# Row numbers in registers: SyncE fetches one tile in every fifth group row by row, in a graph layer's edge sums

## The chip, the cores and the metric

The kernel runs on one core of a Trainium2 chip. The metric is the device time in microseconds of one execution; it is given as the median of three. The five engines of the core are called by the profile's names: PE (matmuls; PEld are its weight loads), DVE, ACT, POOL (GpSimd) and SP (SyncE, which only issues DMAs and waits). A "q" behind an engine's name means its sequencer.

## The reference

One graph layer with 12500 nodes, 256 features and 200000 edges, sorted by destination:

```
h   = relu(layernorm(x))
agg = segment_sum(h[src], dst, 12500)
z   = (1 + eps) * h + agg
t   = relu(batchnorm(z @ W1 + b1))            # 256 -> 512
y   = relu(batchnorm(t @ W2 + b2 + h))        # 512 -> 256
out = x + y
```

The costly part ahead of the two products is `h[src]` with its sum: 200000 rows of 256 features, fetched by number.

## The kernel before, in words

**Tiles and groups.** 128 edges are a tile (1563 of them), and ten tiles a group (`GT`, 157 groups). For most groups POOL fetches the rows of `h` with one indirect DMA for each tile (`gather`, L653, issue at L665). DVE makes for each group a one-hot of destinations (`edges`, L716), and PE multiplies one-hot by rows, ten matmuls into one sum of 128 places (`sums`, L733, matmul at L748). `hold`, `spots`, `put` (L834) and `add` (L851) bring that sum to the right columns of `zc`, where z is built in chunks of 512 nodes. When a chunk is whole, `slice_of` (L861) multiplies it by W1 in four slices, and `take` (L872, L878) stores each slice to `t_tab` from SP (L879), out of one of two places called `ts`.

**Lead-in and table.** In the first 34 steps (`LEAD`) the gathered rows are rows of x, normalised on the core. Beside that the table `h_tab` is written: 2 KB a row, h in a rounded part and the rest. From step 34 on groups gather from `h_tab` into one of three places (`RING`), four steps ahead of their sums (`AHEAD`).

**Counted groups.** Two sets of 12 groups (`SETS`, `JOINT`) are not gathered at all. All of `h_tab` is read in order, in 98 blocks of 128 rows, into a ring of ten places (`h_loads`, the stream loads of SP at L963). A *unit* is one of these groups against eight blocks: DVE makes a one-hot of the high part of the source numbers (`marks`, `mk`, L991), PE multiplies it with a one-hot of the low part (`fill`, L1008), ACT copies the counts (L1012), PE weighs the blocks with them (`weigh`, L1024), and DVE adds the product up (`collect`, L1041). There are 312 units, 13 rounds for each set. The block at which a unit begins moves on by eight in twelve units.

**Homes.** The low one-hots (fp8, ten tiles of 128, 1280 bytes a partition) are made by `low_digits` (L973), one for each group of a set. Their *homes* lie in three places: `away` (three, `AWAY`), `w2s` (three; W2 is loaded later) and `spread` (twelve). The first homes of `spread` also hold the rows of one lead-in group until its sums. The second set takes over homes of the first; `again` and `early_digits` tell at which unit each is made anew. The first set's twelve are made in the last four lead-in steps, three in each.

**Order.** The order on each engine is written out by hand. Steps run through the gathered groups (`line`; the loop of L1175 has steps 34 to 127). `plan` spreads the units over the steps, with budgets for PE and DVE; `early_digits` is one of its costs. A step is a list `works`: units by turns with the group's sums, the placing of earlier sums, and slices. Each engine, SP too, works through its own instructions in the order of the program. SP has, in a step: loads of zc, then, in the places where units and slices stand, stream loads and stores to `t_tab`. A stream load waits until PE has weighed the block that had its place.

Of the kernel before, what the change touches and what calls it, by code (L numbers as in the profile page):

```python
# [9 lines left out]
F32 = mybir.dt.float32  # L10
F32R = mybir.dt.float32r
F8 = mybir.dt.float8e4
I32 = mybir.dt.int32
# [5 lines left out]
P = 128  # L19
# [5 lines left out]
LEAD = 34  # L25
# [7 lines left out]
JOINT = 12  # L33
# [2 lines left out]
PACE = 2  # L36
RINGS = 10
BUSY = 12500
AWAY = 3
EASE = 3  # L40


# [7 lines left out]
def kernel(  # L50
# [16 lines left out]
    nc = tc.nc  # L67
# [311 lines left out]
    def fast():  # L379
# [24 lines left out]
        with ExitStack() as fs:  # L404
# [14 lines left out]
            with ExitStack() as es:  # L419
# [222 lines left out]
                    nc.sync.dma_start(h_cols[g, :, :, :n], hc[:, :, :n])  # L642

                groups = [(t0, min(GT, NTILE - t0)) for t0 in range(0, NTILE, GT)]
                gathered = {i: early[i] for i in range(EARLY)}
                landing = [tc.alloc_semaphore(f"whole{k}") for k in range(AHEAD + 1 + RING)]
                inside = tc.alloc_semaphore("inside")
# [2 lines left out]
                def place_of(i):  # L650
                    return i % (AHEAD + 1) if i < LEAD else AHEAD + 1 + pos[i] % RING

                def gather(i):  # L653
                    t0, n = groups[i]
                    k = i % (AHEAD + 1)
                    if i >= LEAD:
                        pair = rows_pool.tile([P, 2 * GT, D], F32, name="gt")
                        ga = ((0, GT, pair.rearrange("p (t k) d -> p t (k d)", k=2)),)
                    elif k < EARLY:
                        ga = early[k]  # L660
                    else:
                        ga = ((0, GT, singles[k - EARLY]),)
                    for t in reversed(range(t0, t0 + n)):
                        rows = left if t == full_tiles else P
                        fetch = nc.gpsimd.indirect_dma_start(  # L665
                            out=slot(ga, t - t0)[:rows], out_offset=None, in_=x if i < LEAD else h_tab,
                            in_offset=bass.IndirectOffsetOnAxis(ap=srcT[:rows, t : t + 1], axis=0),
                        )
                        if i < NG - 2:
                            tc.no_tile_sem_insts.add(fetch.ins.name)  # L670
                            tc.add_to_no_dep_group(f"rows{i}", fetch.ins)
                            fetch.then_inc(inside if t > t0 else landing[place_of(i)], 16)
                    if i < NG - 2:
                        uses[place_of(i)] += 1
                        arrival[i] = landing[place_of(i)], 16 * uses[place_of(i)]
                    gathered[i] = ga
# [56 lines left out]
                def sums(i, among=()):  # L733

                    t0, n = groups[i]
                    ga, oh = gathered.pop(i), ohs.pop(i)
                    waited = wait_for(i, nc.tensor)
                    ps = sum_place(i)
                    order = list(reversed(range(n)))
                    at = {(k + 1) * n // (len(among) + 1): work for k, work in enumerate(among)}  # L740
                    for k, j in enumerate(order):
                        if k in at:
                            at[k]()
                        rows = left if t0 + j == full_tiles else P
                        lhsT, rhs, to = oh[:rows, j, :], slot(ga, j)[:rows], ps
                        if i >= LEAD:
                            lhsT, rhs, to = lhsT.bitcast(F32R), rhs.bitcast(F32R), ps.rearrange("p k d -> p (k d)")
                        reader = nc.tensor.matmul(to, lhsT=lhsT, rhs=rhs, start=(j == order[0]), stop=(j == order[-1]))  # L748
                        if waited:
                            behind(i, reader)  # L750
                            waited = False
                    summed[i] = ps
# [340 lines left out]
                for i in range(LEAD):  # L1093
                    before = added
                    c_now, c_last, c_next = (chunk_at.get(i + k) for k in (0, -1, 1))
                    gather(line[i + AHEAD])
                    if c_last is not None:
                        turn(c_last)
                    if i + 1 < LEAD:
                        scale("g", i + 1)  # L1100
                    if c_now is not None:
                        scale("c", c_now)
                    edges(line[i + FRONT])
                    if i >= 2:
                        spots(i - 2)
                        hold(i - 2)
                    if i + 1 < LEAD:
                        relus(gathered[i + 1], GT, gathered[i + 1], "g", i + 1)
                    if c_now is not None:
                        h_chunk(c_now)  # L1110
                    if i + 2 < LEAD:
                        look(gathered[i + 2], GT // 2, "g", i + 2)
                        root("g", i + 2)
                    if c_next is not None:
                        look_chunk(c_next)
                        root("c", c_next)
                    for c, f in taken:
                        take(c, f)
                    while added <= i - 4:
                        add(added)  # L1120
                        added += 1
                    if c_last is not None:
                        turn_out(c_last)
                    if c_now is not None:
                        h_halves(c_now)
                    for c in scales.get(i, ()):
                        z_scale(c)

                    def puts():
                        if i >= 3:  # L1130
                            put(i - 3)

                    while touching[whole][-1] < before:
                        queue += [(whole, f) for f in range(HC)]
                        whole += 1
                    taken = queue[:1]
                    queue = queue[1:]

                    def slice_ups():
                        for c, f in taken:  # L1140
                            slice_of(c, f)

                    for n in range(max(JOINT * (i - LEAD + 4) // 4, 0), JOINT * (i - LEAD + 5) // 4):
                        low_digits(n)
                    sums(i, (puts, slice_ups))
                    for c in loads.get(i, ()):
                        z_load(c)
# [27 lines left out]
                for s in range(LEAD, LAST):  # L1175
# [45 lines left out]
                    works = counting[:1] + others[:2]  # L1221
                    for k in range(1, max(len(counting), len(others) - 1)):
                        works += counting[k : k + 1] + others[k + 1 : k + 2]
                    for work in works:
                        work()
                    while whole < NCH and all(k in done for k in touching[whole]):
                        queue += [(whole, f) for f in range(HC)]
                        whole += 1
# [605 lines left out]
```

## Time and profile before

| | |
|---|---|
| median of three runs | 2436.89 us (2431.2, 2436.89, 2457.89) |
| the profiled execution | 2432.64 us, its span 2430.7 us |
| granted TensorE clock, mean | 0.879 |
| HBM read, written | 434.64 MB, 76.80 MB |
| q0, indirect DMAs of POOL: packets, MB, share of 16 engines | 94928, 302.21, 42.5% |
| gathers from h_tab (L665) | 983, 946 ns each |
| matmuls of the gathered sums (L748) | 970, 10 a group |
| units' weighing (L1024) | 2352 matmuls, 445 ns each |

All times are those of one profiled execution. A group row gives a source line, an engine, an operation with out<-in, a count, then busy time, the mean of one, and the engine's idle time just before them with what ended it ("<-issue": nothing that the profile shows). A row by source line gives minimum, median and maximum in ns and the first and last start. A row of the timeline gives start, length, engine, line and operation, and in brackets the idle time before. A row of waits on SP names SP's line, who ended the wait, the total, the number of waits and the longest.

### The profile page before, as it was taken

The page shows a single profiled execution, that of the slowest core. Times are in us where ns is not written, and L with a number is a line of the kernel's source. Part 1 is how long each engine was busy: PE and PEld are TensorE (multiplying, and loading weights), DVE is VectorE, ACT ScalarE, POOL GpSimd, SP SyncE. Part 2 cuts the span into 40 slices and gives each one's busy share as a digit, 9 for nine tenths or more (in the row PEclk, how much of TensorE's full clock was granted, in tenths as well). Part 3 has the DMA queues.
Part 4 walks back from the last instruction along what each step waited for, and adds up shares of the span by engine and source line. Part 5 has one row for each costly group of instructions (what it writes and reads, how often), then busy time and mean ns, then how long its engine had stood idle before and what let it go on. Part 6 is the DMA issues. An engine that isn't in the chain of part 4 may idle for free. (4 is left out here: it accounts for less than half of the span.)

```text
span 2430.7 us, 25628 instructions
## 1 busy us (share of the span) xinstructions
PE 1808.9 (74%) x8988; PEld 1277.0 (53%) x8988; DVE 1445.2 (59%) x2244; ACT 826.6 (34%) x1608; POOL 1332.5 (55%) x1372
## 2 busy tenths in 40 slices
PE   1566666637787788888786788788787877658997
PEld 1444444525565566556554556566565655425445
DVE  4565666636466565565556655555555655544897
ACT  1675656613322222222221222222222222112555
POOL 7666666653565555556545565555555545442550
PEclk9876887868998999899987899999898988689999
DMA  5667677656676766666666676676776756466888
GB/s 165 206 221 237 205 244 222 196 154 198 209 217 201 209 197 209 195 213 203 214 179 190 202 239 205 194 213 201 215 212 198 220 180 219 126 172 218 307 306 335
DMA packets 195410, 513.28 MB, mean 211 GB/s; under 512 B 30358, under 2 KB 45626, under 8 KB 195272
## 3 DMA queue, kind: packets, MB, share of 16 engines
q0 software_dynamic: 94928, 302.21, 42.5%
q1 hardware_dynamic: 98960, 208.29, 25.1%
q8 instruction: 73, 1.20, 0.2%
q10 hardware_dynamic: 1384, 1.06, 0.2%
q14 instruction: 65, 0.53, 0.1%
HBM read 434.64 MB, written 76.80 MB: 210 GB/s over the span
## 5 line engine op out<-in xcount | busy, mean ns | idle before, releaser
L665 POOL DMA_INDIRECT gt<-h_tab,srcT x983 | 930.2, 946 | 786.2 <-PE ps L748 453.4
L1024 PE MATMUL pz<-stream,counts 128*120 128x512 f32 (+1 forms) x2352 | 702.3, 445 | 26.5 <-issue 14.2
L1012 ACT CAST counts<-pm 128x480 fp32r<-128x480 f32 (+1 forms) x600 | 308.2, 556 | 843.9 <-PE pm L1008 387.0
L1024 PEld LDWEIGHTS pz<-stream,counts 128*120 128x120 f32 (+1 forms) x2352 | 453.7, 204 | 136.1 <-issue 17.3
L991 DVE SCALAR_TENSOR_TENSOR mk<-col,dstT 128x960 fp8e4<-128x960 f32 (+5 forms) x328 | 340.8, 1043 | 0.0
L1041 DVE TENSOR_TENSOR gta<-pz,gta 120x512 f32<-120x512 f32 x192 | 132.3, 689 | 325.4 <-PE pz L1024 198.2
L716 DVE TENSOR_TENSOR oh<-col,dstT 128x1280 fp32r<-128x1280 f32 (+1 forms) x131 | 194.2, 1483 | 150.3 <-remote 87.0
L748 PE MATMUL ps<-gt,oh 128*128 128x512 f32 x970 | 259.7, 417 | 0.0
L861 PE MATMUL ph<-zc,w1s 128*128 128x512 f32 (+1 forms) x392 | 207.0, 657 | 49.7 <-issue 19.1
L748 PEld LDWEIGHTS ps<-gt,oh 128*128 128x128 f32 x970 | 199.8, 207 | 49.5 <-issue 1.0
L1008 PE MATMUL pm<-mk,spread 128*128 128x96 fp8e4 (+1 forms) x1560 | 100.9, 210 | 115.8 <-issue 49.8
L1008 PEld LDWEIGHTS <-spread 128*128 128x128 fp8e4 x1560 | 79.8, 101 | 170.4 <-issue 109.9
L878 ACT COPY ts<-ph 128x512 f32<-128x512 f32 x96 | 56.0, 584 | 331.5 <-issue 176.4
L1041 DVE TENSOR_TENSOR gtb<-pz,gtb 120x512 f32<-120x512 f32 x96 | 66.1, 689 | 152.5 <-PE pz L1024 94.5
L665 POOL DMA_INDIRECT stream<-in_x_dram,srcT x130 | 124.3, 956 | 57.4 <-issue 28.8
L851 DVE TENSOR_TENSOR zc<-pz,zc 128x512 f32<-128x512 f32 (+15 forms) x227 | 110.4, 513 | 72.1 <-PE pz L834 38.0
L861 PEld LDWEIGHTS ph<-zc,w1s 128*128 128x128 f32 x392 | 81.4, 214 | 124.8 <-issue 80.6
L872 DVE BATCH_NORM_STATS2 st<-ph 128x6 f32<-128x512 f32 x96 | 66.8, 696 | 132.1 <-PE ph L861 63.3
L834 PE MATMUL pz<-at,zh 128*128 128x256 f32 (+2 forms) x484 | 100.0, 318 | 56.2 <-issue 16.9
L834 PEld LDWEIGHTS pz<-at,zh 128*128 128x128 f32 (+1 forms) x484 | 79.4, 206 | 89.1 <-issue 39.7
L665 POOL DMA_INDIRECT gta<-in_x_dram,srcT x96 | 92.7, 966 | 50.4 <-issue 17.3
L1008 PE MATMUL pm<-mk,away 128*128 128x96 fp8e4 (+1 forms) x780 | 52.8, 215 | 74.2 <-DVE mk L991 33.3
(247 smaller groups left out, 2271.6 us busy)
## 6 DMA issues: line engine op xcount, KB each, us to landing
stream<-h_tab SPq DMA_DIRECT2D x201, 256.0 KB
h_tab<-gt SPq DMA_DIRECT2D x24, 1024.0 KB
t_tab<-ts SPq DMA_DIRECT2D x96, 256.0 KB
gt<-h_tab,srcT POOLq DMA_INDIRECT x983
gt<-in_x_dram SPq DMA_DIRECT2D x24, 512.0 KB
h_cols<-gt SPq DMA_DIRECT2D x24, 512.0 KB
zc<-h_cols SPq DMA_DIRECT2D x24, 512.0 KB
yT<-h_cols SPq DMA_DIRECT2D x24, 512.0 KB
```

What stands on the lines that cost most here:

```text
L665: fetch = nc.gpsimd.indirect_dma_start(out=slot(ga, t - t0)[:rows], out_offset=None, in_=x if i < LEAD else h_tab, in_offset=bass.Indirect ...
L716: nc.vector.tensor_tensor(oh.bitcast(F32R) if i >= LEAD else oh, col[:, :P].unsqueeze(1).to_broadcast([P, n, P]), dstT[:, t0 : t0 + n].uns ...
L748: reader = nc.tensor.matmul(to, lhsT=lhsT, rhs=rhs, start=(j == order[0]), stop=(j == order[-1]))
L834: nc.tensor.matmul(pz[:, d, :n], lhsT=zs[:rows, k, d * P : (d + 1) * P].bitcast(F32R), rhs=at[:rows, :n].bitcast(F32R), start=(k == 0), st ...
L851: nc.vector.tensor_add(side, pz[:, :, a - lo : b - lo], side)
L861: nc.tensor.matmul(ph[:, :n], lhsT=w1s[:, d, f * P : (f + 1) * P], rhs=zc[c][:, d, :n], start=(d == 0), stop=(d == DC - 1),)
L872: nc.vector.bn_stats(st1[:, f, c, :], ph[:, :n])
L991: nc.vector.scalar_tensor_tensor(mk[:, :, done * WIN : done * WIN + w], col[:, :w].unsqueeze(1).to_broadcast([P, GT, w]), float(a0 * WIN), ...
L1008: nc.tensor.matmul(pm[:, k, :], lhsT=digits[z][j][:, t0 + k, :], rhs=marked[n][:, t0 + k, :w], start=True, stop=True,)
L1012: nc.scalar.copy(counts[n][:, :nb, :].bitcast(F32R).rearrange("p a (t d) -> p t a d", d=WIN)[:, t0 : t0 + m], pm.rearrange("p t (a d) -> p ...
L1024: nc.tensor.matmul(products[n][:ROWS], lhsT=counts[n][:rows, k, :].bitcast(F32R), rhs=ring[(b0 + k) % len(ring)][:rows].bitcast(F32R), sta ...
L1041: nc.vector.tensor_add(acc[j][:ROWS], got, acc[j][:ROWS])
```

## The change

`AWAY` goes from 3 to 0 and the space goes to two places called `apart` of one tile of 2 KB rows each. `alone` picks every fifth gathered group from step 42 on, up to step 126. Of such a group the first tile (j = 0) is no longer gathered by POOL. Instead SP fetches its 128 rows, each with a DMA of its own, over the five steps that begin six steps ahead of the sums: 28 rows in a step (`ASK`), dealt out behind each piece of the step's work. For that the tile's 128 row numbers are loaded at the start into a row of `vrows`, and at the head of each step the 28 numbers due go into registers of SP. Two semaphores count the landings; PE waits for 128 of them ahead of that tile's matmul, the last of the group's ten.

With 15 homes instead of 18, `cut` is 3 instead of 6, and `again` has nine homes that are taken over instead of six. The first set's low one-hots are made 2, 2, 3 and 5 in the last four lead-in steps.

```diff
-AWAY = 3
+AWAY = 0
+GAP = 5
+ASK = 28
...
+                alone = {line[s]: k for k, s in enumerate(range(LEAD + 8, LAST - 1, GAP))}
+                assert len(alone) <= VN and GAP * ASK >= P
+                numbers = vrows.bitcast(I32)
+                for i, k in alone.items():
+                    first = groups[i][0] * P
+                    nc.sync.dma_start(
+                        numbers[k : k + 1, :], src[first : first + P].rearrange("(o e) -> o e", o=1)
+                    )
+                apart_sem = [tc.alloc_semaphore(f"apart{k}") for k in range(2)]
+                places_apart, at_row, asked = {}, {}, {}
+
+                def rows_apart(s, part, parts_):
+
+                    for i, k in alone.items():
+                        begin = pos[i] - GAP - 1
+                        if not begin <= s < begin + GAP:
+                            continue
+                        if i not in places_apart:
+                            places_apart[i] = wide.tile([P, 2 * D], F32, name="apart", bufs=2)
+                            at_row[i] = 0
+                        if part == 0:
+                            known = range(ASK * (s - begin), min(P, ASK * (s - begin + 1)))
+                            _, values = nc.values_load_multi_w_load_instructions(
+                                numbers[k : k + 1, known[0] : known[-1] + 1], engines=[mybir.EngineType.SP],
+                                min_val=0, max_val=N - 1,
+                                skip_runtime_bounds_check_because="src holds row numbers of x",
+                            )
+                            asked.update(zip(known, values))
+                        a, upto = at_row[i], min(P, ASK * (s - begin) + ASK * (part + 1) // parts_)
+                        at_row[i] = max(a, upto)
+                        for p in range(a, upto):
+                            value = asked.pop(p)
+                            row_in = nc.sync.dma_start(
+                                places_apart[i][p : p + 1, :], h_tab[bass.ds(value, 1), :]
+                            )
+                            tc.no_tile_sem_insts.add(row_in.ins.name)
+                            tc.add_to_no_dep_group(f"apart{i}", row_in.ins)
+                            row_in.then_inc(apart_sem[k % 2], 16)
+
...
-                    for t in reversed(range(t0, t0 + n)):
+                    t_end = t0 + (i in alone)
+                    for t in reversed(range(t_end, t0 + n)):
...
-                            fetch.then_inc(inside if t > t0 else landing[place_of(i)], 16)
+                            fetch.then_inc(inside if t > t_end else landing[place_of(i)], 16)
...
+                        lonely = j == 0 and i in alone
+                        if lonely:
+                            assert at_row[i] == P
+                            nc.tensor.wait_ge(apart_sem[alone[i] % 2], 16 * P * (alone[i] // 2 + 1))
+                            rhs = places_apart.pop(i).bitcast(F32R)
...
-                    for n in range(max(JOINT * (i - LEAD + 4) // 4, 0), JOINT * (i - LEAD + 5) // 4):
-                        low_digits(n)
+                    clear = min(cut + len(homes) - after, JOINT)
+                    made = [clear * k // 3 for k in range(4)] + [JOINT]
+                    if i >= LEAD - 4:
+                        for n in range(made[i - LEAD + 4], made[i - LEAD + 5]):
+                            low_digits(n)
...
-                    for work in works:
+                    for k, work in enumerate(works):
                         work()
+                        rows_apart(s, k, len(works))
```

More of the change, by code (lines that the diff above doesn't have):

```diff
@@ L747, in sums @@
                             lhsT, rhs, to = lhsT.bitcast(F32R), rhs.bitcast(F32R), ps.rearrange("p k d -> p (k d)")
-                        reader = nc.tensor.matmul(to, lhsT=lhsT, rhs=rhs, start=(j == order[0]), stop=(j == order[-1]))
+                        lonely = j == 0 and i in alone
[3 more added lines that the diff above has]
+                            rhs = places_apart.pop(i).bitcast(F32R)
+                        reader = nc.tensor.matmul(to, lhsT=lhsT, rhs=rhs, start=(j == order[0]), stop=(j == order[-1]))
+                        if lonely:
+                            tc.declare_no_dep(
+                                reader.ins, group=f"apart{i}", reason="its engine waits for the rows' semaphore"
+                            )
+                            tc.declare_fence(reader.ins, group=f"apart{i}")
                         if waited:
```

## The prediction

> **What bounds the kernel now.** First the page's head, for the shares, and then one window over the stretch in which both kinds of groups are worked (566.8 to 2090 us). The change lies almost wholly in it.
>
> ```profile
> span 2430.7 us, 25628 instructions
> PE 1808.9 (74%) x8988; PEld 1277.0 (53%) x8988; DVE 1445.2 (59%) x2244; ACT 826.6 (34%) x1608; POOL 1332.5 (55%) x1372
> q1 hardware_dynamic: 98960, 208.29, 25.1%
> ```
>
> ```profile
> 566.80:2090.00 1523.20, 1223.40 (x6977) 893.66 (x6975) 870.15 (x1222) 395.97 (x802) 842.07 (x890) 0.90 0.68 206
> ```
>
> In order, behind the stretch's length: busy time of PE, PEld, DVE, ACT and POOL, the granted TensorE clock, the share of DMA and GB/s. PE is busy 1223 of 1523 us (80%), POOL 842 (55%). The next question is who ends PE's idle time, and POOL's; the groups of instructions from 600 to 2090 us tell it in their last columns (idle before, and its releasers).
>
> ```profile
> L665 POOL DMA_INDIRECT gt<-h_tab,srcT x870 | 823.1, 946 | 662.7 <-PE ps L748 364.5 <-issue 238.5 <-PE pz L834 27.5
> L748 PE MATMUL ps<-gt,oh 128*128 128x512 f32 x860 | 223.5, 408 | 0.0
> L1008 PE MATMUL pm<-mk,spread 128*128 128x96 fp8e4 (+1 forms) x1560 | 100.9, 210 | 115.8 <-issue 49.8 <-DVE mk L991 42.1 <-ACT counts L1012 22.4
> ```
>
> The matmuls that read the gathered rows (L748) have 0.0 us of idle time before them: PE never waits for a gather in this stretch. Its idle time stands before the small count matmuls, ended by DVE's one-hots and ACT's copies. POOL is the one that waits: 364.5 us for PE to free a place. How much room that leaves, one group shows in the timelines of POOL and PE:
>
> ```profile
> 1196.43 0.94 POOL L665 DMA_INDIRECT gt<-h_tab,srcT  x1 [4.66 <-PE ps L748]
> 1197.68 0.95 POOL L665 DMA_INDIRECT gt<-h_tab,srcT  x1 [0.30 <-issue]
> ...
> 1207.69 0.95 POOL L665 DMA_INDIRECT gt<-h_tab,srcT  x1 [0.30 <-issue]
> ```
>
> ```profile
> 1193.71 2.45 PE L748 MATMUL ps<-gt,oh 128*128 128x512 f32 x10
> 1208.74 2.44 PE L748 MATMUL ps<-gt,oh 128*128 128x512 f32 x10
> 1231.38 2.48 PE L748 MATMUL ps<-gt,oh 128*128 128x512 f32 x10
> 1244.00 2.46 PE L748 MATMUL ps<-gt,oh 128*128 128x512 f32 x10
> ```
>
> The sums that end at 1196.16 free a place; POOL starts ten gathers into it at 1196.43, one each 1.25 us (0.95 and 0.30 of issue), and is done at 1208.64. With three places, these rows are read by the third sums from there, at 1244.00: 35 us after POOL's end. So a gather of 12.5 us serves a step of about 17 us and is ready two steps early. **The stretch is paced by PE with its handoffs to DVE and ACT, and gathers are off that path.**
>
> The step's length and the work of SP, which gets the new job:
>
> ```profile
> L748 PE MATMUL ps<-gt,oh x970: 387/393/802, 566.8 to 2208.9; 128*128 128x512 f32 x194
> ```
>
> ```profile
> L963 SPq DMA_DIRECT2D stream<-h_tab x203: 319/320/687, 563.6 to 2065.6; - x102
> ```
>
> ```profile
> SPq L963 <- PE pz L1024: 490.5, 94, 14.4
> SPq L879 <- ACT ts L878: 150.5, 19, 29.6
> SPq L963 <- PE pm L1008: 138.0, 19, 10.4
> SPq L963 <- remote: 137.7, 21, 13.0
> ```
>
> 970 matmuls, ten a group, are 97 groups in 1642 us: 16.9 us a step. SP's own DMAs in that time are 203 stream loads of 0.32 us and, of these two rows of the page, most:
>
> ```profile
> t_tab<-ts SPq DMA_DIRECT2D x96, 256.0 KB
> zc<-h_cols SPq DMA_DIRECT2D x24, 512.0 KB
> ```
>
> At 0.32 each, (203 + 96 + 24) x 0.32 is about 100 us. Nearly all else is waiting, 917 us in these four rows alone (window 566.8 to 2090).
>
> **The change part by part.** *Removed from POOL.* The loop takes steps 42, 47, ... 122: 17 tiles by its bounds, not 18. Each takes one indirect DMA of 1.25 us off a group: 17 x 1.25 = 21 us of POOL. In the stretch POOL gets to wait 21 us longer for PE; gain on the path 0. If gathers paced these steps it would be all 21 us, and that is the other bound.
>
> *Added to SP.* For each tile 128 row DMAs of 2 KB, 2176 in all, each from a row number in a register; five steps a tile, 28 rows in four of them and 16 in the last, dealt out behind each piece of a step's work. 17 x 5 = 85 of 94 steps carry them. No row of the trace is a DMA with a register's address, or a load of 28 registers. The nearest are the one-row loads of L225 with a fixed address, the flag's load into one register, and a branch:
>
> ```profile
> L225 SPq DMA_DIRECT2D rawi_d<-in_dst_dram x2: 223/223/223, 2.4 to 7.4; - x2
> L225 SPq DMA_DIRECT2D rawi_s<-in_src_dram x2: 234/242/251, 8.2 to 8.5; - x2
> ```
>
> ```profile
> L1799 SPq TENSOR_LOAD <-flag x1: 470/470/470, 28.0 to 28.0; - x1
> ```
>
> ```profile
> L1800 SPq COMPARE_BRANCH  x2: 43/44/44, 28.5 to 2423.6; - x2
> ```
>
> A row costs SP its DMA, its share of the register load and the address arithmetic. Lower bound: 0.223 + 0.470/28 + nothing = 0.24 us. Upper: the 0.32 of a 128-row load, a whole 0.470 for each register and four instructions of 0.044 = 0.97. I take 0.24 for the DMA (nearest in shape: one row), 0.10 for the register (one call loads 28, so a fifth of a lone load, as an estimate) and two instructions of 0.044: **0.43 us, 12 us in a step of 28 rows**. What SP can bear: 85 steps x 16.9 = 1437 us, less 100 of its own, over 2176 rows: **0.61 us a row**. At 0.43 it fits, with 5 us a step left (16.9 - 12.0), of which its own DMAs take a good 1.
>
> SP works in order, so what is queued behind a batch of rows matters: the stream loads (for PE's weighing, L1024), t_tab's stores (they free ts for ACT) and zc's loads. A ring place is refilled once its last reader is done; ten places against eight blocks a unit, and block numbers advance 8 in 12 units, so a new block is first read three units later. 312 units run over 90 steps, 3.5 a step or 4.9 us each: **about 14.7 us from release to first use**, and a batch at 0.43 (28 rows over some eight pieces of work, 1.5 us, ahead of the step's first with the register load, 3 + 1.5) uses a third of it. ts has two places for about one slice a step, so a store may come a step late. At these costs the path sees 0; if the cover goes, the loads are what is late next, and PE stands before L1024.
>
> [...]
>
> *Added to PE.* One wait ahead of the lone tile's matmul, 17 in all, each like this one:
>
> ```profile
> L834 PEldq EVENT_SEMAPHORE  x114: 51/51/51, 579.7 to 2184.0; - x114
> ```
>
> 17 x 0.051 = 0.9 us; bounds 0 and 17 x 0.4 (a whole matmul of L748) = 7. The rows of a tile are issued by step pos - 2 and read in step pos, a step of spare.
>
> *One-hots with three homes fewer.* Their number stays 24. In the last four lead-in steps 2, 2, 3, 5 are made instead of 3 each, and at the change of sets nine within 12 units instead of six within six; three move there from units 72 to 96. The lead-in's last step, by DVE and PE's weight loads:
>
> ```profile
> 557.63 4.28 DVE L973 TENSOR_TENSOR spread<-col,srcT 128x1280 fp8e4<-128x1280 f32 x3
> ...
> 564.87 2.21 DVE L991 SCALAR_TENSOR_TENSOR mk<-col,dstT 128x960 fp8e4<-128x960 f32 x2
> ```
>
> ```profile
> 566.07 0.77 PEld L1008 LDWEIGHTS <-away 128*128 128x128 fp8e4 x10 [9.15 <-DVE mk L991]
> ```
>
> Three take 4.28 us on DVE, whose next mk ends a 9.15 us wait of PE. Two more there cost 2 x 1.43 = **+2.9 us**, on the path. The steps relieved of one give back between 0 and 2.9; I take 0. At the change of sets three more cost 0 to 4.3, given back earlier; I take 0 on balance. The planner's due times shift with the one-hots; by its own arithmetic all units still end in step 123, some steps getting one unit more and others one less: 0, within 10 us either way.
>
> *At the start.* 17 loads of 512 B for the row numbers stand ahead of the first x loads on SP:
>
> ```profile
> 8.23 0.53 SPq L225 DMA_DIRECT2D rawi_s<-in_src_dram x2
> 33.09 4.19 SPq L402 DMA_DIRECT2D gt<-in_x_dram  x4
> ```
>
> At 0.27 apiece (L225's two in 0.53) they take 4.6 us, in a gap in which SP waits from the flag's load at 28.0 until 33.09: 0.2 us, and 4.6 if they can't start before.
>
> *On the DMA engines.* Bytes are the same. A q1 packet takes 0.251 x 16 x 2430.7 / 98960 = 99 ns.
>
> **Sum**: +0.9 + 2.9 + 0.2 + 0 = +4 us. The profiled execution took 2432.64 us beside its span of 2430.7, so 2436.6 on its footing; the median of the three runs is 2436.89, 4.3 above it, so I forecast **2441 us** for the median, and 2425 to 2462 for this case alone.
>
> **The rivals.** *SP becomes the bound* (slower). Place: the register load and row DMAs of a step. Point: 0.61 us a row; beyond it rows, stream loads and stores all fall behind and every 0.01 us costs 2176 x 0.01 = 22 us. If each register costs a whole 0.470, a row is 0.71: 1545 + 100 - 1437 = 208 us more, about **2650**; at 0.64 it is 56 more, about 2500. For it: the unseen part of a row's price is as large as the seen one. Against: one call loads 28 registers, and it needs half again what I take.
>
> *The relief of POOL counts*: 2441 - 21 = **2420**, more if fewer software-queue DMAs also speed others. Against: 0.0 us before L748.
>
> *One DMA engine carries all rows* (slower). If every row went to the same one of the 16, that engine would get 2176 x 99 ns = 215 us within 1437, 15% beside the mean share of 0.68, so 0.83; its free part falls from 0.32 to 0.17, and every transfer that is spread over all engines ends with it. A load's 128 packets are 8 x 99 ns = 0.8 us of each engine; doubled, that is still well inside 14.7. Where it broke through, by a third of a microsecond a step for 94 steps, it would be +31: **2472**. [...] No view here tells engines apart.
>
> *It doesn't do what it says*: were rows late, PE would wait at the lone tile; that is the first rival's end, and counted there.
>
> **How the numbers follow.** No change 0.62; SP the bound 0.24, some 0.10 of it under 2560; POOL's relief 0.09, half of it past 1%; one DMA engine 0.05. 1% is 24 us, about what a measurement of this kernel tells from none (its three runs span 2431.2 to 2457.89). Faster by over 1%: 0.05; slower: 0.24 + 0.05 = 0.29; within: 0.66. The range, 2418 to 2560, leaves out 0.04 below and 0.14 above.
>
> **What would show it.** Right: L665 with 966 gathers from h_tab, its idle for L748 up by about 20 us; L748 still at 0 idle; SP's waits of L963 shrunk, row DMAs of 0.22 to 0.32 us; five one-hots in a row before the first mk. Wrong: PE idle before L1024 or the lone matmul ended by DMA, SP with no waits left, steps of 20 us; or L748's gathers found on the chain and a stretch shorter by 20 us.

## The result, and the profile after

| | before | after |
|---|---|---|
| median, same chip | 2440.75 us (5 runs, 2431.2 to 2457.89) | 2754.54 us (5 runs, 2728.26 to 2771.24) |
| span of the profiled execution | 2430.7 us | 2752.7 us |

The ratio is **1.1245, 95% interval 1.1169 to 1.1322**: slower by 314 us. The forecast was 2441 and the range ended at 2560. What happened is the rival called *SP becomes the bound*, and more of it than its price had foreseen.

The page's head after, and the stretch in which rows are fetched (columns as before):

```profile
span 2752.7 us, 32248 instructions
PE 1883.6 (68%) x8988; PEld 1327.9 (48%) x8988; DVE 1444.3 (52%) x2244; ACT 831.9 (30%) x1608; POOL 1320.4 (48%) x1355
```

```profile
560.00:2373.00 1813.00, 1267.27 (x6769) 925.79 (x6769) 851.88 (x1183) 392.52 (x784) 806.45 (x853) 0.83 0.57 169
```

PE is busy 70% of the stretch, where it was 80%, and its granted clock is 0.83 where it was 0.90. DMA carries less (0.57 for 0.68). Nothing is at its limit in this row, because SP's own work isn't counted as busy. The groups from 600 to 2373 us, then the weighing of before (600 to 2090 us), and the gathered sums of the whole run after:

```profile
L707 POOL DMA_INDIRECT gt<-h_tab,srcT x828 | 782.8, 945 | 986.0 <-PE ps L795 744.5 <-issue 226.7 <-PE pm L1060 7.4
L1076 PE MATMUL pz<-stream,counts 128*120 128x512 f32 (+1 forms) x2242 | 731.1, 476 | 52.0 <-DMA stream<-h_tab 27.0 <-issue 23.5 <-DVE gtb L1093 0.9
L795 PE MATMUL ps<-gt,oh 128*128 128x512 f32 x824 | 220.3, 416 | 0.7 <-issue 0.7
L795 PE MATMUL ps<-apart,oh 128*128 128x512 f32 x16 | 6.3, 397 | 0.0
L1060 PE MATMUL pm<-mk,spread 128*128 128x96 fp8e4 (+1 forms) x2170 | 153.6, 220 | 329.7 <-issue 176.8 <-ACT counts L1064 82.1 <-DVE mk L1043 70.1
L1060 PE MATMUL pm<-mk,w2s 128*128 128x96 fp8e4 (+1 forms) x720 | 52.3, 224 | 112.8 <-issue 54.2 <-DVE mk L1043 29.8 <-ACT counts L1064 28.6
```

```profile
L1024 PE MATMUL pz<-stream,counts 128*120 128x512 f32 (+1 forms) x2301 | 686.4, 445 | 17.8 <-issue 12.1 <-ACT counts L1012 5.1 <-DVE gta L1041 0.6
```

```profile
L795 PE MATMUL ps<-gt,oh x953: 387/393/796, 559.5 to 2531.6; 128*128 128x512 f32 x191
```

(L707 is L665 of before, L795 is L748, L1076 is L1024, L1060 is L1008, L1064 is L1012, L1093 is L1041, L1015 is L963, L931 is L879.) The gathered sums still wait for nothing (0.7 us), the 16 lone matmuls of this window neither (0.0), and POOL waits for PE twice as long as before (744.5 us): gathers are further off the path. New is the DMA that ends PE's waits ahead of the weighing, the stream loads: 27.0 of 52.0 us, where no DMA stood before. But most of PE's new idle time stands elsewhere: ahead of the count matmuls (the two L1060 lines) it went from 244 us to 442, ended half by nothing that the profile shows and half by ACT's copies and DVE's one-hots. 953 matmuls of the gathered sums and the 17 lone ones are 97 groups of ten; in 1972 us (559.5 to 2531.6) that is 20.3 us a step, and it was 16.9.

SP is the engine to look at. First what a row costs it, one kind of instruction to a line of the view (FUSED_REGOPS and MOVE are taken for the address arithmetic and a register move: e4, with fixed row numbers, has neither):

```profile
L679 SPq FUSED_REGOPS  x2176: 2/37/1397, 596.8 to 2373.4; - x198
L679 SPq MOVE apart<-h_tab x2176: 2/29/1396, 596.9 to 2373.4; - x198
L679 SPq DMA_DIRECT2D apart<-h_tab x2176: 2/228/1402, 597.0 to 2373.5; - x198
```

```profile
L669 SPq TENSOR_LOAD <-vrows x85: 204/1841/2440, 594.4 to 2359.8; - x85
```

Then what SP waits for from 566.8 to 2373 us (before, these waits came to over 900 us):

```profile
SPq L1015 <- PE pz L1076: 14.0, 21, 2.4
SPq L931 <- ACT ts L930: 10.0, 1, 10.0
SPq L1015 <- PE pm L1060: 9.8, 17, 2.9
SPq L931 <- ACT zh L861: 8.5, 3, 8.0
SPq L1015 <- remote: 8.3, 5, 5.6
SPq L669 <- DMA stream<-h_tab: 3.4, 2, 1.9
SPq L931 <- ACT counts L1064: 2.4, 8, 0.4
```

These lines come to 56 us, and 33 us of waits fall into the 1776 us from the first row to the last (597.0 to 2373.5): **SP is full.** From each instruction's start to the next one's, SP's own loads, stores and waits take 156 us of these; 1620 us are left for 2176 rows, **0.745 us each**: 0.679 for the three instructions and 0.066 for the register. The medians, 37 + 29 + 228 ns, would never show this. The maxima do: a MOVE, 29 ns in the median, took up to 1396. Here is SP around one of POOL's bursts, and below it the burst (start, length, count):

```profile
1301.79 5.73 SPq L679 DMA_DIRECT2D apart<-h_tab  x8
1307.53 0.00 SPq L1015 DMA_DIRECT2D stream<-h_tab  x1
1308.96 8.86 SPq L679 DMA_DIRECT2D apart<-h_tab  x12
1318.26 0.37 SPq L1015 DMA_DIRECT2D stream<-h_tab  x1
1318.82 1.47 SPq L679 DMA_DIRECT2D apart<-h_tab  x4
1320.39 0.36 SPq L1015 DMA_DIRECT2D stream<-h_tab  x1
```

```profile
1300.46 0.94 POOL L707 DMA_INDIRECT gt<-h_tab,srcT  x1 [10.32 <-PE ps L795]
...
1311.70 0.95 POOL L707 DMA_INDIRECT gt<-h_tab,srcT  x1 [0.30 <-issue]
1322.92 0.94 POOL L707 DMA_INDIRECT gt<-h_tab,srcT  x1 [10.27 <-PE ps L795]
```

While POOL issues its ten gathers, 0.3 us apart, a *burst* (1300.46 to 1312.65), eight rows take 5.74 us, **0.72 each**. Later, between two bursts, four rows take 1.57 us, **0.39 each**. Over the whole run, from a row's start to the next instruction after its DMA, rows begun inside POOL's bursts cost 0.95 us on average (46% of them) and the others 0.45. Single instructions show it without exception: of the 6528 that make up the rows, 540 took over 0.6 us, and all 540 began in a burst or within 1.5 us behind one; of the 3386 others none took over 0.3.

Late next are the stream loads (the last two lines: what waited for them, us and times):

```profile
L1015 SPq DMA_DIRECT2D stream<-h_tab x203: 2/363/1398, 556.3 to 2393.5; - x102
...
  PEld pz L1076: 46.4, 16
  PE pz L1076: 38.7, 12
```

Paired block by block with the first matmul that reads it, a load starts 11.5 us or more ahead of its use in the kernel before (median 19.8), and after the change as little as 2.6 us ahead (median 13.2); stores to `t_tab` start on average 12.5 us after their copy (600 to 2100 us), where it was 0.03. PE's granted clock went down as its waits grew: 0.83 at 70% busy in the stretch above, where it was 0.90 at 80%. Three windows of the same stretch (the third number from the right is the granted clock):

```profile
1302.30:1309.10 6.80, 3.48 (x27) 2.35 (x26) 1.97 (x3) 0.56 (x1) 5.07 (x6) 1.00 0.82 256
1309.20:1319.30 10.10, 6.86 (x28) 5.03 (x28) 4.55 (x7) 2.88 (x6) 2.84 (x3) 0.50 0.45 139
1319.50:1333.00 13.50, 9.67 (x68) 7.59 (x67) 5.38 (x8) 2.14 (x4) 7.64 (x9) 1.00 0.71 221
```

PE was busy half of the first window (3.48 of 6.80 us), and in the next its clock is half: 28 matmuls in 10.1 us. The clock fell at 1309.16, 2.0 us into an idle stretch of PE of 3.83 us (1307.17 to 1311.00), and rose at 1319.40, 8.4 us after PE had begun again, with a gap of 1.44 us between.

### The profile page after: what moved, and what is told of

It reads as the page before. It is cut to its first block, busy times and chain, and to the rows that moved or that the text cites. A ratio compares the mean times of both kernels' runs of the same rounds, so it can differ in the third digit from the quotient of the medians.

```text
span 2752.7 us, 32248 instructions
## 1 busy us (share of the span) xinstructions
PE 1883.6 (68%) x8988; PEld 1327.9 (48%) x8988; DVE 1444.3 (52%) x2244; ACT 831.9 (30%) x1608; POOL 1320.4 (48%) x1355
## 5 line engine op out<-in xcount | busy, mean ns | idle before, releaser
L707 POOL DMA_INDIRECT gt<-h_tab,srcT x966 | 913.4, 946 | 1122.7 <-PE ps L795 837.8
L1076 PE MATMUL pz<-stream,counts 128*120 128x512 f32 (+1 forms) x2352 | 769.8, 477 | 63.3 <-issue 28.7
L1064 ACT CAST counts<-pm 128x480 fp32r<-128x480 f32 (+1 forms) x600 | 310.5, 555 | 1135.4 <-PE pm L1060 464.2
L1076 PEld LDWEIGHTS pz<-stream,counts 128*120 128x120 f32 (+1 forms) x2352 | 496.7, 223 | 191.6 <-DMA stream<-h_tab 33.8
L1060 PE MATMUL pm<-mk,spread 128*128 128x96 fp8e4 (+1 forms) x2340 | 162.9, 218 | 339.4 <-issue 181.7
L1093 DVE TENSOR_TENSOR gta<-pz,gta 120x512 f32<-120x512 f32 x192 | 132.1, 688 | 459.9 <-remote 198.2
L1060 PEld LDWEIGHTS <-spread 128*128 128x128 fp8e4 x2340 | 127.0, 105 | 424.5 <-issue 313.6
L795 PE MATMUL ps<-gt,oh 128*128 128x512 f32 x953 | 261.2, 424 | 0.7 <-issue 0.7
L795 PEld LDWEIGHTS ps<-gt,oh 128*128 128x128 f32 x953 | 202.8, 213 | 51.9 <-issue 1.4
L1093 DVE TENSOR_TENSOR gtb<-pz,gtb 120x512 f32<-120x512 f32 x96 | 66.0, 688 | 227.7 <-remote 140.7
L707 POOL DMA_INDIRECT stream<-in_x_dram,srcT x130 | 126.4, 973 | 60.6 <-issue 30.9
L1060 PE MATMUL pm<-mk,w2s 128*128 128x96 fp8e4 (+1 forms) x780 | 55.8, 222 | 122.2 <-issue 54.2
L886 PE MATMUL pz<-at,zh 128*128 128x256 f32 (+2 forms) x484 | 90.7, 305 | 54.7 <-issue 30.1
L707 POOL DMA_INDIRECT gta<-in_x_dram,srcT x96 | 92.8, 966 | 51.7 <-issue 19.7
L1060 PEld LDWEIGHTS <-w2s 128*128 128x128 fp8e4 x780 | 43.8, 107 | 150.9 <-issue 98.3
```

The costliest lines, as they stand in the source:

```text
L707: fetch = nc.gpsimd.indirect_dma_start(out=slot(ga, t - t0)[:rows], out_offset=None, in_=x if i < LEAD else h_tab, in_offset=bass.Indirect ...
L886: nc.tensor.matmul(pz[:, d, :n], lhsT=zs[:rows, k, d * P : (d + 1) * P].bitcast(F32R), rhs=at[:rows, :n].bitcast(F32R), start=(k == 0), st ...
L1060: nc.tensor.matmul(pm[:, k, :], lhsT=digits[z][j][:, t0 + k, :], rhs=marked[n][:, t0 + k, :w], start=True, stop=True,)
L1064: nc.scalar.copy(counts[n][:, :nb, :].bitcast(F32R).rearrange("p a (t d) -> p t a d", d=WIN)[:, t0 : t0 + m], pm.rearrange("p t (a d) -> p ...
L1076: nc.tensor.matmul(products[n][:ROWS], lhsT=counts[n][:rows, k, :].bitcast(F32R), rhs=ring[(b0 + k) % len(ring)][:rows].bitcast(F32R), sta ...
L1093: nc.vector.tensor_add(acc[j][:ROWS], got, acc[j][:ROWS])
```

## The experiments

Theory at the start: SP's time is used up, because its rows stall while POOL issues gathers. Rivals: the row DMAs load a DMA engine or the memory; the new homes or the order of work cost time; rows cost time by themselves wherever SP stands. Ratios are to the kernel before on the same chip: its median was 2560.23 us for the first four kernels, 2434.57 for the fifth to eighth, 2545.44 for the ninth to twelfth and 2555.41 for the last two.

### The parts of the change

**Relief and homes without rows** (e1_relief_only):

```diff
-                        rows_apart(s, k, len(works))
...
-                            rhs = places_apart.pop(i).bitcast(F32R)
+                            rhs = slot(ga, 1)[:rows].bitcast(F32R)
```

> The changed kernel without SP's row DMAs, register loads and PE's 17 waits; POOL still gathers one tile less in 17 groups, and the homes and the one-hots' order stay changed. The lone tile's rows are left out: its matmul reads the rows of the tile beside it. Theory 'SP is the bound' (SP's issuing fills the steps at 0.75 us a row): all of the loss goes, 2425 to 2455, like before. Rival 'one DMA engine carries all rows': the same, since the rows are gone. Rival 'homes and order' (moved one-hots, shifted planner): most of the loss stays, over 2600. If POOL's relief is worth something by itself, 2420 or less.

2531.5 us, ratio 0.9877 [0.9823, 0.9932]. The rest of the change does not cost; it gains a little. Two more runs, on another chip, part that gain. First the homes alone (e11_homes_only):

```diff
-                alone = {line[s]: k for k, s in enumerate(range(LEAD + 8, LAST - 1, GAP))}
+                alone = {}
```

> The changed kernel's homes and low one-hots with no row and no tile taken off GpSimd, so the whole computation as before. Theory 'homes and their order cost about what was reckoned, 3 us': 0.998 to 1.004. If the homes were the gain of the kernel without rows: 0.985 to 0.99.

2546.82 us, 1.0012 [0.9974, 1.005]: nothing. And e1's kernel again (e12_relief_again):

> The first kernel again (homes changed, 17 gathers fewer, no rows: those tiles are left out), beside the homes alone. Theory 'a gather costs the others about 0.47 us' (970 gathers against 97 plain ones were worth 452 us): 17 of them are 8 us, 0.996 to 0.998 of the homes alone, plus what a wait on a freed place gave in the first measurement, 0.985 to 0.995 of before. Theory 'gathers off the path cost nothing': as the homes alone, within 0.003.

2535.03 us, 0.9964 [0.9933, 0.9995]. Homes and order are worth nothing that can be measured. Seventeen gathers fewer are worth 0.4% on this chip and 1.2% on the first, 10 and 29 us, though nobody waits for a gather.

### SP's time, or the row DMAs

**Half the rate** (e2_half_rate), eight tiles instead of 17:

```diff
-GAP = 5
-ASK = 28
+GAP = 10
+ASK = 14
...
-                alone = {line[s]: k for k, s in enumerate(range(LEAD + 8, LAST - 1, GAP))}
+                alone = {line[s]: k for k, s in enumerate(range(LEAD + 13, LAST - 1, GAP))}
```

> The changed kernel with a tile in every tenth group and 14 rows a step over ten steps: 8 tiles, 1024 rows. Theory 'SP is the bound': 14 rows at 0.75 us are 10.5 us of a step of 16.9, so SP keeps up and all of the loss goes: 2430 to 2470. A cost that goes with the number of rows, whatever it is (one DMA engine's time among them): 1024 of 2176 rows, so 2441 + 0.47 x 314 = 2590.

2678.04 us, 1.0465 [1.0398, 1.0532]. SP now waits again (600 to 2100 us, the two longest):

```profile
SPq L1015 <- remote: 163.8, 32, 8.8
SPq L1015 <- PE pz L1076: 143.9, 65, 9.9
```

Stream loads start 12.6 us or more ahead of their use, as before; 11 stores are over 1 us late, up to 8.7. **So "SP is full" is not the whole of it**: at half the rate SP isn't, and 4.7% are still lost.

**Short rows** (e3_short_rows), 64 bytes of each 2 KB, same count; the lone matmul has 16 columns and stands last but one of its group:

```diff
-places_apart[i][p : p + 1, :], h_tab[bass.ds(value, 1), :]
+places_apart[i][p : p + 1, :16], h_tab[bass.ds(value, 1), :16]
```

> The changed kernel with 64 B of each row instead of 2 KB: same count of row DMAs, register loads and waits. 496 of 512 values of each lone row are left out, and its matmul has 16 columns. Theory 'SP is the bound': SP's instructions are the same, so the loss stays: 2700 to 2770. Rival 'one DMA engine carries all rows': its packets shrink 32 times in bytes, the loss goes: 2440 to 2500.

2796.11 us, 1.0956 [1.0885, 1.1027], a row at 0.68 us of SP. A packet of 64 bytes took a DMA engine 8 ns, one of 2 KB 84 (medians), and the loss stays large: neither the bytes nor one loaded DMA engine are the price.

**Fixed rows** (e4_fixed_rows), no register load and no address arithmetic, the same number of DMAs from row numbers written into the program:

```diff
-                            _, values = nc.values_load_multi_w_load_instructions(
...
+                            asked.update((p, (997 * (128 * k + p)) % N) for p in known)
```

> The changed kernel with row numbers known to the program: no register load, no register instruction, the same 2176 row DMAs of 2 KB. It fetches other rows than asked for. Theory 'SP is the bound': a row costs 0.28 us and the stalls; with as much stall a row as in the changed kernel (0.27) 0.55 us, under the limit of 0.61, so most of the loss goes: 2440 to 2520. If the stalls come with each instruction of SP, fewer instructions mean fewer stalls, and it is 2440. Rival 'one DMA engine carries all rows': the same DMAs, so the loss stays, 2700 to 2770.

2644.98 us, 1.0343 [1.0292, 1.0393]. A row costs 0.33 us here:

```profile
L674 SPq DMA_DIRECT2D apart<-h_tab x2176: 2/252/1424, 603.3 to 2245.6; - x198
```

Without the registers and the arithmetic, that is with less of SP's time, the 9.6% of the kernel above fall to 3.4%. Another loss stays, as at half the rate: 4.5% and 5.8% against the kernel without rows on the same chip (2531.5 us), with stream loads on time, and stores too but for the 11 at half the rate. How it shows is in ACT's waits ahead of the copies of counts, here of the kernel before, of e1, of half the rate, and of the changed kernel (fixed rows: 383 us):

```profile
ACT counts L1012 <- remote: 149.3, 32, 8.4
```

```profile
ACT counts L1062 <- remote: 229.1, 58, 7.3
```

```profile
ACT counts L1064 <- remote: 389.8, 75, 11.6
```

```profile
ACT counts L1064 <- remote: 429.2, 99, 10.8
```

"Remote" means here that the semaphore's update which ended the wait came 1.5 us or more after the end of any recorded instruction of PE that raises it. PE has worked, but is heard late. No missing record explains it: each of these traces has all 3120 count matmuls. In the kernel before the 32 updates came 1.8 us behind that end (median), at most 5.1, and in the changed kernel the 99 came 2.9 us behind it, at most 8.5. The first and the last of these four lines are of one chip, the two between of another, on which e1's 229 us is the value without rows.

**SP's time without DMAs** (e5_sp_loads_half, e6_sp_loads_full): register loads in place of rows.

```diff
-                            row_in = nc.sync.dma_start(
...
+                        for _ in range(LOADS * (part + 1) // parts_ - LOADS * part // parts_):
+                            nc.values_load_multi_w_load_instructions(
```

> No row DMAs: in each of the steps that carried rows SyncE loads 28 registers five times instead (at 1.84 us a load about 9 us of SyncE a step, what 28 rows cost with fixed addresses), and the lone matmul reads another tile of its group, so that the rows of 17 tiles are left out. Theory 'SyncE's time': stream loads and stores are still on time at this occupancy, so the time is that of the kernel without rows, a ratio of 0.98 to 1.00. Theory 'any work between SyncE's waits costs': 1.03 to 1.05, as with half the rows or fixed addresses. If it is 0.98 to 1.00, what those two kernels lost comes from the row DMAs and not from SyncE's occupancy.

> As the one before with eleven loads of 28 registers a step, about 20 us of SyncE, what 28 rows took in the changed kernel (28 x 0.745 = 20.9); rows of 17 tiles left out, no row DMA at all. Theory 'SyncE is the bound': stream loads come late and the step grows to SyncE's time, 20 us and a ratio of 1.06 to 1.12, without one row being moved. Theory 'the row DMAs disturb the others': no more than 1.02.

1.0035 [0.9992, 1.0077] and 1.0189 [1.0101, 1.0276]. Both miss their question: no instruction used the loaded numbers, and the built program holds no such load, only 425 and 935 more semaphore instructions on SP. These have something to tell themselves (e6):

```profile
L666 SPq EVENT_SEMAPHORE  x935: 2/17/717, 595.6 to 2101.9; - x187
```

Their median is 17 ns, and 70 of the 557 that began in POOL's bursts or within 1.5 us behind took over 0.4 us; none of the other 378 did. So the stall needs neither a row DMA nor a register, only instructions on SP. That it makes up the 1.9% of e6 isn't shown.

### POOL's indirect DMAs

**Plain group DMAs with rows** (e7_plain_gathers) and **without** (e8_plain_no_rows):

```diff
+                        fetch = nc.gpsimd.dma_start(
+                            ga[0][2][:, t_end - t0 : n, :],
+                            h_tab[b : b + m * P, :].rearrange("(t p) d -> p t d", p=P),
+                        )
```

> The changed kernel with its row DMAs, but from step 34 on GpSimd fetches the other nine or ten tiles of a group with one DMA of consecutive rows instead of one indirect DMA a tile (other data, the same bytes), so GpSimd issues for a few us less a step. Theory 'GpSimd's issuing of indirect DMAs stalls SyncE': a row falls from 0.68 to about 0.41 us, 11.5 us a step, SyncE waits again, ratio to before 0.97 to 1.03. Theory 'the traffic or SyncE itself makes the row dear': a row stays at 0.65 to 0.75 us and the ratio at 1.07 or more.

> Control for the one before: plain group DMAs from step 34 on and no rows (the lone matmul reads another tile). Gathers were off the path, so 0.96 to 1.00 of before. The difference between the two is what 2176 rows cost when GpSimd issues no indirect DMAs: 0 to 2% if a row costs 0.41 us and SyncE's time is all, 4% or more if the row DMAs disturb the compute engines whatever GpSimd does.

2126.49 us, 0.8723 [0.8657, 0.8789], and 1982.05 us, **0.8131** [0.8067, 0.8195]. The rows of e7 first:

```profile
L679 SPq FUSED_REGOPS  x2176: 37/37/51, 557.7 to 1773.5; - x198
L679 SPq MOVE apart<-h_tab x2176: 29/29/38, 557.8 to 1773.5; - x198
L679 SPq DMA_DIRECT2D apart<-h_tab x2176: 224/228/973, 557.8 to 1773.6; - x198
```

No MOVE takes more than 38 ns. A row costs 0.41 us from start to start. It still costs 7% against e8, since the steps without rows are now 12 us and SP is full again at 28 x 0.41 + 1.8 for the registers + its own loads: its waits from 600 to 1700 us add up to 41 us, where e8 has 1006.

The surprise is e8. Taking away the indirect DMAs, for which nobody waits, takes 19% off the time. From 600 to 1700 us, e8 and under it the kernel before:

```profile
600.00:1700.00 1100.00, 1049.15 (x6731) 784.41 (x6730) 867.33 (x1241) 371.87 (x765) 83.90 (x87) 0.98 0.79 270
```

```profile
600.00:1700.00 1100.00, 884.29 (x5025) 644.45 (x5026) 637.66 (x894) 289.37 (x586) 612.18 (x647) 0.91 0.68 205
```

PE is busy 95% of the time instead of 80%, at a clock of 0.98, and does 6731 matmuls where it did 5025. More bytes move a second. No wait of ACT for counts is "remote" any more.

**Plain, half the rows** (e9_plain_half_rate): the edits of e2 and e7 together.

> The kernel with plain group DMAs (other data) and half the rows: 8 tiles, 14 rows a step. At 0.41 us a row and 1 us for the registers SyncE needs about 7 us of rows in a step of 12.2 us and waits again. Theory 'rows cost only where SyncE is full': the time of the kernel with plain group DMAs and no rows, a ratio to before of 0.81 to 0.83, stream loads started at their slot's release. Theory 'each row costs about the same wherever SyncE stands', as between the full and the half rate in the first runs: half of the 5.9% between those two plain kernels, 0.84 to 0.86.

1985.48 us, 0.78 [0.7757, 0.7844]. That is on another chip than e8, so the ratios can't be set side by side; in absolute time it comes to e8's 1982.05 us, and e14 below, plain and without rows on a third chip, takes 1983.55. SP waits, stream loads are on time, and ACT's row has only PE's recorded ends (whole run):

```profile
ACT counts L1074 <- PE pm L1070: 496.7, 230, 4.6
```

So 1024 rows cost nothing that shows where SP has time and POOL issues no indirect DMAs. The 4.7% of half the rate need both, the rows and the indirect DMAs.

**Consecutive rows, still indirect** (e10_consecutive), the kernel before:

```diff
+        in_turn = consts.tile([P, 8], I32, name="in_turn")
+        nc.gpsimd.iota(in_turn, pattern=[[P, 8]], base=0, channel_multiplier=1)
...
-ap=srcT[:rows, t : t + 1]
+ap=srcT[:rows, t : t + 1] if i < LEAD else in_turn[:rows, t % 8 : t % 8 + 1]
```

> The kernel before with every indirect DMA kept, but from step 34 on the row numbers it reads are consecutive (128 rows in a run, other data), so that the traffic is that of the plain group DMAs and the issuing that of before. Theory 'GpSimd's issuing of indirect DMAs holds back the others': as before, 0.97 to 1.01, and matmul results still announced late. Theory 'scattered rows hold back the DMA engines': toward the plain group DMAs, 0.81 to 0.88.

2539.12 us, 0.9959 [0.9915, 1.0003]. It isn't the scatter.

**The changed kernel with that edit** (e13_rows_consecutive):

> The changed kernel with all its row DMAs and all its indirect DMAs, the indirect ones reading consecutive rows from step 34 on (other data). Theory 'issuing indirect DMAs stalls SyncE': a row stays at 0.65 to 0.72 us and the time at the changed kernel's, a ratio to before of 1.08 to 1.13. Theory 'scattered reads stall SyncE's row DMAs': a row near 0.41 us, SyncE waits again, ratio 1.03 or less.

2787.81 us, 1.0882 [1.0813, 1.0952]; rows stall as in the changed kernel (0.69 us for the three instructions), and SP waits 33 us from 600 to 2100 us:

```profile
L681 SPq MOVE apart<-h_tab x2176: 2/29/1412, 613.9 to 2424.1; - x198
```

**Ten plain DMAs a group** (e14_ten_plain), the kernel before with one plain DMA for each tile:

```diff
+                        if LEAD <= i < NG - 2:
+                            fetch = nc.gpsimd.dma_start(slot(ga, t - t0)[:rows], h_tab[t % 8 * P : t % 8 * P + rows, :])
```

> The kernel before with ten plain DMAs a group on GpSimd instead of ten indirect ones, one a tile, from step 34 on (consecutive rows, other data). Theory 'the number of DMAs that GpSimd issues holds back the others': near before, 0.95 to 1.00. Theory 'making the row addresses of an indirect DMA does it': near one plain DMA a group, 0.78 to 0.84.

1983.55 us, **0.7754** [0.7712, 0.7796], as with one DMA a group. POOL's rows of e10 and e14:

```profile
L667 POOL DMA_INDIRECT gt<-h_tab,in_turn x983 | 930.0, 946 | 892.8 <-PE ps L752 558.2
```

```profile
L666 POOL DMA_DIRECT2D gt<-h_tab x970 | 512.6, 539 | 720.7 <-PE ps L751 701.4
```

Count, bytes and addresses are the same in these two, but for the 13 tiles of the last two groups, which stay indirect in e14; both pages have 94928 packets and 302.21 MB on queue q0. What differs is that one is indirect. It takes POOL 946 ns for 539, and it is what holds back the others: e10 takes 0.9959 of before, e14 0.7754.

## Why the prediction was wrong, point by point

**The count of tiles, the order of one-hots, PE's extra wait: right.** 966 gathers and 2176 rows; PE had no idle time ahead of any of the 17 lone matmuls. The last one-hots of the lead-in and the first mk:

```profile
547.52 7.07 DVE L1025 TENSOR_TENSOR spread<-col,srcT 128x1280 fp8e4<-128x1280 f32 x5
557.56 2.21 DVE L1043 SCALAR_TENSOR_TENSOR mk<-col,dstT 128x960 fp8e4<-128x960 f32 x2
```

Five in a row, as forecast; with the homes alone the time is 1.0012 of before.

**POOL's relief at 0: wrong by a little.** It was priced by who waits for a gather, and nobody does. But gathers delay others (e8): 970 of them were worth 2434.57 - 1982.05 = 452 us, 0.47 each. Seventeen would be 8 us by that, and 10 and 29 us were measured.

**The limit of 0.61 us a row: right.** With the measured 0.745 the rival's own rule gives 2441 + 2176 x (0.745 - 0.61) = 2735; the time is 2754.54. That it comes so near may be luck in part: the rule has no term for the second loss (4.5% and 5.8% where SP isn't full), and whether a full SP hides that loss isn't shown. What is late next, stream loads and stores, was right too, and the signs named for being wrong came: SP without waits, steps of 20 us. That PE would stand before L1024 was right in part only: its idle time there grew by 34 us, ahead of the count matmuls by 198.

**The price of a row, 0.43 us: here it failed.** The sum has no term for stalls. Its parts are near for an undisturbed row: 0.228 for the DMA (taken at 0.24), 0.066 for arithmetic (0.09), 0.066 for the register (0.10). With 0.12 us between the instructions, which the sum left out too, that is 0.48 us, and it would have fitted under 0.61. The other 0.27 us of the measured 0.745 are stalls beside POOL's indirect DMAs, which run for 57% of the time from 600 to 2373 us; in and just behind them single SP instructions, register moves too, take 0.7 or 1.4 us. e7 shows the price where they are gone, e13 that it is not the scatter.

The rows that set the price could not have shown this. Three of L225's four DMAs stood among POOL's first indirect DMAs (3.1 to 28.1 us) and took 223 to 251 ns, and of the stream loads of before 113 of 203 began inside bursts, at a median of 320 ns and 418 at most (the 687 of that row began outside). What differs is how much SP does there. From 600 to 2090 us, in and within 1.5 us behind bursts, SP ran 361 instructions before the change and one took over 0.6 us; e6 ran 910 and 94 did; the changed kernel, register loads aside, 2809 and 483 did. So the step that failed is the price of lone issues put on 28 rows a step; why the stalls come only when SP does more is open.

**"Beyond 0.61 only": wrong.** Below the limit the rows were taken to cost nothing. Half the rate and fixed rows stay below it and cost 4.7% and 3.4%. e9 shows that this too needs the indirect DMAs.

**The rivals.** SP the bound is what came. That a row is one packet is so: the changed kernel has 2176 more packets of 2 KB. That all rows go to one DMA engine was the author's assumption, and which engine a row took no run shows; as the cause it falls with e3 (64-byte rows still lose 9.6%) and e9 (no loss).

Open: by what path an indirect DMA on POOL holds back SP's instructions and the announcements of PE's results. The runs show that it does (e8: 0.8131), that addresses (e10: 0.9959), bytes and count (e14: 0.7754) are not it, and that rows on SP make it worse (PE's late updates: 32 before, 99 after); not where they meet. Nor is the way from SP's lateness to PE's idle time ahead of the count matmuls followed wait by wait. A kernel that computes the reference and beats both was not found: the gathers need row numbers, and the plain DMAs of e7, e8, e9 and e14 fetch consecutive rows, other data than asked for.

## What to carry to other kernels

Price an instruction from rows that stand beside the same neighbours and come as densely, and look at the maximum beside the median: here SyncE's lone loads beside GpSimd's indirect DMAs were not held up (418 ns at most inside bursts), and a dense run of small DMAs had twice its price there (0.95 us a row for 0.45). Where no such row exists, a short run of the instruction in the kernel gives the price. An engine for which nobody waits can still be the dear one, as GpSimd here (e8: 0.8131); a kernel that leaves its work out (other data, same bytes) shows it in one run. And a DMA queue that still has waits is not yet free: at half the rate of small DMAs (e2) SyncE waited again, and 4.7% were lost.

## What the runs showed of the hardware

- Replacing 970 indirect DMAs of GpSimd by plain ones, one or ten a group, took 19 to 22% off a kernel in which PE never waited for a gather (0.8131 and 0.7754, on two chips), and PE's granted clock from 600 to 1700 us was 0.98 where it was 0.91.
- While GpSimd issued indirect DMAs, a 29 ns register move of SyncE took up to 1396 ns; with plain DMAs 38 ns at most. All 540 instructions of the rows that took over 0.6 us began in a burst of indirect DMAs or within 1.5 us behind it. A 17 ns semaphore instruction took up to 717 ns there, with no row DMA in the kernel.
- Beside indirect DMAs, the semaphore updates of TensorE that ended 32 of 280 waits of ScalarE came 1.5 to 5.1 us behind the end of the last recorded instruction that raises it; with SyncE's rows 99 of 326 did, up to 8.5 us; with plain DMAs none of 230 and 221.
- A row DMA of SyncE with its address in a register: 228 ns of issue, 0.41 us from one row to the next undisturbed; 28 registers from SBUF in 1.84 us.
- An indirect DMA of 128 rows of 2 KB took GpSimd 946 ns, a plain one 539.
